# Gate convolution and output projection of a two-layer image block: which operand the matrix engine holds, and which it streams

## The chip, the cores and the metric

One Trainium2 chip, of which the kernel uses one core. The metric is the device time of one execution, in microseconds (us). Five timed runs of the kernel before are given, and one profiled execution of it. The engines are named as in the profile: PE is the matrix engine (PEld its loads of the stationary operand), DVE the vector engine, ACT the engine for activation functions, POOL a second vector engine, and SP issues nearly all DMAs.

## The reference

The input x has 16 images of 256 channels and 32 x 32 positions. Two layers act on each image, with residual connections and group norms around them. The first is attention (4 heads of 32) with a feed-forward part, the second is a selective scan over the 1024 positions, gated by a short convolution. Only the end of the second layer matters for this change:

```python
ctx = sigmoid(conv1d(xp, gate_w, padding=1) + gate_b)   # 3 taps, 256 -> 256 channels
...
y = scan(...) + u * D                                   # 512 channels, 1024 positions
y = y * silu(z)
x_mamba = y @ out_proj_w.T                              # 512 -> 256 channels
return (x_mamba * ctx).reshape(B, C, H, W)              # (positions, channels), read as (channels, H, W)
```

The last line is a bare reshape of an array of 1024 positions x 256 channels into 256 rows of 1024. Row r of the output therefore holds positions 4r to 4r + 3, each with its 256 channels. All matrix products here are in f32.

## The kernel before, in words

An SBUF or PSUM tile has 128 partitions. A matrix instruction holds a stationary tile (up to 128 x 128) in PE and streams a moving tile (up to 512 columns) through it; the columns of the stationary tile become the partitions of the result in PSUM. In the calls below the stationary operand is the second argument of `nc.tensor.matmul`, the moving one the third.

Activations lie with channels on partitions and positions along the tile. The gated result is wanted with position groups on partitions (row r has positions 4r to 4r + 3). So the kernel before makes every fourth position of the activations the stationary operand, 128 of them at a time (`ds(first, P, 4)`), and streams the weights, 256 output channels wide. The result comes out with positions on partitions. This is done in two places. `gate(o, hf, q, k)` (L707) convolves: three taps for each half of the input channels, then a one-row product that adds the bias (L713), then a tanh on ACT, and `g` is written to the DRAM tile `gs`. The sigmoid is taken as 0.5 (1 + tanh(x / 2)). `gate_and_store` (L887) does the output projection: four products, one for each 128 of the 512 channels, for each of eight groups of 128 positions, into the PSUM tile `m_ps`. `finish` then multiplies on DVE by (1 + g) (L874) and adds a quarter of the product to the residual `xs` (L876); the quarter holds both halves, of the sigmoid and of the silu. A finished row block goes to `out` by DMA.

The scan is the main loop. It has 4096 units, 256 for each image. Unit n runs one scan of 128 x 1024 on DVE (`scan`, L950), whose decay `a` was made two units ahead by two small products on PE (L942) and an exponential on ACT (L944), and whose input `dub` was multiplied on POOL (L933). There are two PSUM buffers for `a`, so the products for unit n + 2 wait until scan n has ended. `outputs` contracts each finished group of eight units on PE (`yb`, L975, and the turn at L987). Everything else is side work, written as generators that yield a share; between units the loop advances the side work by about one step of share 1 to 1.5. While image b is scanned, the side work is: the first norm of image b + 1 and the loads for the gate of image b - 1, then `gate_and_store(b - 1)`, then the attention and the scan inputs of image b + 1. `scan_inputs` holds the gate convolution: for each of four blocks d, two taps of the depthwise convolution on DVE (L693) with a projection `u_ps` on PE (L679), then four steps that each hold one call of `gate`. On each engine the instructions run in the order in which the program wrote them. SP's queue is separate and in order.

PSUM tiles come from few banks: `psum3` goes round three (two of pool `mm`, one of `accp`). `hwork` takes one of four SBUF tiles of 128 x 512, which the norms and the scan inputs use too.

Of the kernel before, what the change touches and what calls it, by code (L numbers as in the profile page):

```python
# [50 lines left out]
def attention_then_scan_kernel(  # L51
# [91 lines left out]
    gate_b = const.tile([1, C], F32, name="gate_b")  # L143
    nc.sync.dma_start(gate_b, gate_bias)
    one_row = const.tile([1, P], F32, name="one_row")
    nc.vector.memset(one_row, 1.0)
# [467 lines left out]
    def scan_inputs(b):  # L614
# [84 lines left out]
        def gate(o, hf, q, k):  # L699
            if (hf, q, k) == (0, 0, 0):  # L700
                gates["g"] = work("g")
            if (q, k) == (0, 0):
                gates["ps"] = psum("g_ps")
            g, ps = gates["g"], gates["ps"]
            first = o * HL + hf * 2 + q
            for t in range(3):
                nc.tensor.matmul(  # L707
                    ps[:, ts(q, C)], xp[k][:, ds(first + t, P, 4)], wg_s[:, k, t, :],
                    start=(k == 0 and t == 0), stop=False,
                )  # L710
            if k < KC - 1:
                return
            nc.tensor.matmul(ps[:, ts(q, C)], one_row, gate_b, start=False, stop=True)  # L713
            if q == 1:
                table("tanh")
                nc.scalar.activation(g[:, hs(hf)], ps, AF.Tanh, scale=0.5)
# [8 lines left out]
        for d in range(ND):  # L725
# [8 lines left out]
            gate(d // 2, d % 2, 0, 0)  # L734
            yield 1
            gate(d // 2, d % 2, 0, 1)
# [4 lines left out]
            gate(d // 2, d % 2, 1, 0)  # L741
            yield 1
            gate(d // 2, d % 2, 1, 1)
# [107 lines left out]
    def gate_and_store(b):  # L851
# [18 lines left out]
        ready = []  # L870

        def finish():
            for o, hf, ps in ready:
                nc.vector.scalar_tensor_tensor(ps, gs[o][:, hs(hf)], 1.0, ps, ALU.add, ALU.mult)  # L874
# [4 lines left out]
            ready.clear()  # L879

        for o in range(KC):
            for hf in range(2):
                ps = psum3("m_ps")
                for q in range(2):
                    first = o * HL + hf * 2 + q
                    for d in range(ND):
                        nc.tensor.matmul(  # L887
                            ps[:, ts(q, C)], us[d][:, ds(first, P, 4)], wo_s[:, d, :],
                            start=(d == 0), stop=(d == ND - 1),
                        )  # L890
                    if q == 1:
                        finish()
                    if come:
                        come.pop(0)()
# [252 lines left out]
```

## Time and profile before

| what | value |
|---|---|
| median of five runs | 12741.91 us |
| lowest and highest of the five | 12673.7 and 12773.79 us |
| the profiled execution | 12770.75 us, its span 12769.0 us |
| DVE busy | 11316.9 us, of which scans (L950) 9204.3 us |
| POOL busy | 10014.4 us |
| PE busy | 9939.5 us |
| gate products (L707), busy on PE | 461.1 us (tile `g_ps`), bias rows (L713) 87.3 us |
| output projection (L887), busy on PE | 320.6 us |
| mean granted clock of PE | 0.796 |

The profile is of one execution. Busy time is the union of an engine's instructions, so overlapped records count once. A granted clock of 1.00 is PE's full speed, and 0.50 half. Idle time of an engine says what it waited for, not that the wait costs run time: an engine that is not the bound may wait for nothing. Times in the timeline are microseconds from the start of the span.

### The profile page before, as it was taken

What the parts mean: (1) busy time and instruction counts of PE and PEld (TensorE: products, weight loads), DVE (VectorE), ACT (ScalarE), POOL (GpSimd) and SP (SyncE); (2) the same over time, 40 slices, a digit from 0 to 9 for tenths busy, and PEclk for the clock granted to TensorE, in tenths of its full rate; (3) what the DMA queues carried; (4) which work ended last, traced back from release to release, by engine and by line L of the source; (5) the groups of instructions that cost most, each with busy time, mean ns of one, the idle gap of its engine ahead of it and who ended that gap; (6) DMA issues with size and microseconds to landing.
All of it is one profiled execution on the core that took longest, in us unless ns stands there. A gap on an engine that the chain in (4) does not pass through costs nothing.

```text
span 12769.0 us, 424578 instructions
## 1 busy us (share of the span) xinstructions
PE 9939.5 (78%) x186800; PEld 5503.2 (43%) x186800; DVE 11316.9 (89%) x7480; ACT 7505.2 (59%) x10726; POOL 10014.4 (78%) x4201
## 2 busy tenths in 40 slices
PE   6676977868788787986878778697786878868777
PEld 2344444444444444444444444444444444444444
DVE  2789999989989899798998999999998998989998
ACT  3565665656556565465656656565565665656554
POOL 0587878878788787687878878787887878878798
PEclk8787988869788787687878878797787978878756
DMA  1567666676666766467666676666767667676676
GB/s 54 184 218 242 213 221 237 221 243 214 220 239 220 244 220 231 174 218 247 218 224 235 220 239 219 236 221 215 235 222 244 212 220 240 214 246 208 228 251 229
DMA packets 1038404, 2820.12 MB, mean 221 GB/s; under 512 B 290370, under 2 KB 368451, under 8 KB 1036548
## 3 DMA queue, kind: packets, MB, share of 16 engines
q1 hardware_dynamic: 1036548, 2792.97, 64.0%
q8 instruction: 1459, 23.90, 0.8%
q14 instruction: 397, 3.25, 0.1%
HBM read 2513.82 MB, written 261.62 MB: 217 GB/s over the span
## 4 chain that ended last, share of the span: by engine, by line
PE 40%; DVE 29%; issue 12%; ACT 8%; DMA 6%; POOL 3%; SPq 1%; DVEq 0%; POOLq 0%; ACTq 0%
DVE h L950 22%; PE yb L975 8%; PE s_ps L449 7%; PE a L942 6%; ACT a L944 4%; DMA dub<-dus 3%; PE av L508 3%; POOL dub L933 3%; PE st_ps L520 3%; PE yb L987 2%; PE z_ps L657 2%; PE g_ps L707 2%; PE m_ps L887 2%; DVE u L693 1%; DMA xs<-ud 1%
## 5 line engine op out<-in xcount | busy, mean ns | idle before, releaser
L933 POOL TENSOR_TENSOR dub<-dub,bt 128x1024 f32<-128x1024 f32 x4096 | 9789.1, 2420 | 2625.4 <-DMA dub<-dus 2457.4
L950 DVE TENSOR_TENSOR_SCAN h<-a,dub 128x1024 f32<-128x1024 f32 x4096 | 9204.3, 2276 | 721.9 <-ACT a L944 410.2
L944 ACT ACTIVATE a<-a,acol 128x1024 f32<-128x1024 f32 x4096 | 4464.1, 1090 | 3083.7 <-PE a L942 2957.7
L975 PEld LDWEIGHTS yb<-h,cd 128*32 128x32 f32 x131072 | 2509.7, 129 | 2688.3 <-issue 1304.2
L942 PE MATMUL a<-pieces,pick 48*128 48x512 bf16 x8192 | 1915.4, 459 | 2228.3 <-DVE h L950 2113.0
L975 PE MATMUL yb<-h,cd 128*32 128x64 f32 x131072 | 3282.5, 253 | 339.3 <-ACT y L981 231.8
L942 PEld LDWEIGHTS <-pick 48*128 48x128 bf16 x8192 | 570.9, 95 | 2636.4 <-issue 2226.2
L981 ACT COPY y<-yb 128x256 f32<-128x256 f32 x2048 | 763.9, 373 | 742.9 <-PE yb L975 734.5
L508 PE MATMUL av<-pt,vv 128*64 128x512 f32 x2048 | 606.4, 673 | 2.6 <-ACT sums L497 1.7
L528 ACT ACTIVATE pt<-st_ps 128x512 f32<-128x512 f32 x1024 | 553.8, 597 | 76.9 <-PE st_ps L520 75.8
L987 PE MATMUL yb<-turn,y 128*32 128x16 f32 x32768 | 590.9, 214 | 4.3 <-issue 3.3
L520 PE MATMUL st_ps<-sp 33*128 33x512 f32 x2048 | 586.1, 648 | 3.3 <-ACT pt L528 3.3
L449 PE MATMUL s_ps<-kd,q 32*64 32x512 f32 x2044 | 565.5, 641 | 17.1 <-DVE mx L428 9.0
L987 PEld LDWEIGHTS yb<-turn,y 128*32 128x32 f32 x32768 | 572.9, 159 | 5.3 <-issue 3.6
L449 PE MATMUL s_ps<-k,q 32*64 32x512 f32 x2048 | 540.5, 615 | 0.0
L991 ACT COPY yo<-yb 128x128 f32<-128x128 f32 x512 | 135.7, 265 | 594.5 <-PE yb L987 586.2
L428 DVE CUSTOM_DVE_ANT_0 over<-s_ps,over 128x512 f32<-128x512 f32 x512 | 343.3, 672 | 137.5 <-issue 60.4
L707 PE MATMUL g_ps<-w,xp 128*128 128x256 f32 x1464 | 461.1, 455 | 0.0
L707 PEld LDWEIGHTS g_ps<-w,xp 128*128 128x128 f32 x1464 | 370.2, 326 | 69.0 <-issue 58.6
L454 ACT ACTIVATE over<-s_ps 128x512 f32<-128x512 f32 x511 | 303.5, 594 | 60.5 <-PE s_ps L449 60.5
L693 DVE SCALAR_TENSOR_TENSOR u<-up,cwh,u 128x1024 f32<-128x1024 f32 x192 | 312.9, 1630 | 28.0 <-ACT u L685 27.7
L887 PE MATMUL m_ps<-w,xs 128*128 128x256 f32 x1024 | 320.6, 463 | 10.9 <-POOL xs L862 10.9
(178 smaller groups left out, 7110.0 us busy)
## 6 DMA issues: line engine op xcount, KB each, us to landing
dub<-dus SPq DMA_DIRECT2D x4096, 512.0 KB
dps<-pc SPq DMA_DIRECT2D x384, 128.0 KB
pieces<-dps SPq DMA_DIRECT2D x1024, 48.0 KB
xs<-in_x_dram SPq DMA_DIRECT2D x64, 512.0 KB
xs<-kept SPq DMA_DIRECT2D x64, 512.0 KB
zs<-z SPq DMA_DIRECT2D x64, 512.0 KB
ud<-u SPq DMA_DIRECT2D x64, 512.0 KB
dus<-du SPq DMA_DIRECT2D x64, 512.0 KB
```

The source lines that it names most:

```text
L449: nc.tensor.matmul(s[ts(e, 64)], q4[r, ts(c, 64)], keys[r], start=True, stop=True)
L508: nc.tensor.matmul(av[ts(e, 2 * DH)], vv[j // (NJ // 2)][:, j % (NJ // 2), 2 * pair + e, :], pts[e], start=(j == 0), stop=(j == NJ - 1),)
L520: nc.tensor.matmul(s, ka[r, ts(j, P)], qa[r, hs(hf)], start=True, stop=True)
L707: nc.tensor.matmul(ps[:, ts(q, C)], xp[k][:, ds(first + t, P, 4)], wg_s[:, k, t, :], start=(k == 0 and t == 0), stop=False,)
L887: nc.tensor.matmul(ps[:, ts(q, C)], us[d][:, ds(first, P, 4)], wo_s[:, d, :], start=(d == 0), stop=(d == ND - 1),)
L933: nc.gpsimd.tensor_tensor(v, v, blocks[units[n][0]]["bt"], ALU.mult)
L942: nc.tensor.matmul(a[:, hs(hf)], w, pieces[r], start=True, stop=True)
L944: nc.scalar.activation(a, a, AF.Exp, scale=acol[:, at : at + 1])
L950: nc.vector.tensor_tensor_scan(now["h", e][:, i, :], decays.pop(n), loaded.pop(n), 0.0, ALU.mult, ALU.add)
L975: nc.tensor.matmul(yb[ts(g, 32), ts(s, 64)], cd[:, at // 16, ts(c, 32)], hbuf[:, :, at : at + 8], start=(c == 0), stop=(c == 1),)
L981: nc.scalar.copy(y2[:, r], yb[:, :256])
L987: nc.tensor.matmul(some[ts(r, 32), x], y2[:, r, x:256:8], turn[:, x], start=True, stop=True)
```

## The change

In both places the operands are exchanged. The weights become the stationary operand and 512 neighbouring positions are streamed, so that results come out with channels on partitions. In the gate this halves the number of products, and the bias becomes a column that ACT adds within the tanh, halved beforehand because the activation's scale of 0.5 does not reach the bias. `gs` then holds channels on rows. In the output projection each step projects 512 positions to 128 channels; `join` multiplies by (1 + g) on DVE into an SBUF tile, still by channels; `turn_back` takes every fourth position of two joined tiles as the stationary operand and streams a 128 x 128 identity, which puts position groups on partitions; `finish` adds the quarter to the residual. The eight steps of the stage keep their yields; four are now projections and four are turns, in a written order.

```diff
@@ -140,10 +140,9 @@
         assert i + n <= w
         return vec[:, o + i : o + i + n]
 
-    gate_b = const.tile([1, C], F32, name="gate_b")
-    nc.sync.dma_start(gate_b, gate_bias)
-    one_row = const.tile([1, P], F32, name="one_row")
-    nc.vector.memset(one_row, 1.0)
+    gate_b = const.tile([P, KC], F32, name="gate_b")
+    nc.sync.dma_start(gate_b, gate_bias.rearrange("o (k p) -> p (o k)", p=P))
+    nc.vector.tensor_scalar(gate_b, gate_b, 0.5, None, ALU.mult)
     ident = const.tile([P, P], F32, name="ident")
     make_identity(nc, ident)
     avg = const.tile([P, P], F32, name="avg")
@@ -696,24 +695,22 @@
 
         gates = {}
 
-        def gate(o, hf, q, k):
-            if (hf, q, k) == (0, 0, 0):
+        def gate(o, hf, part):
+            if (hf, part) == (0, 0):
                 gates["g"] = work("g")
-            if (q, k) == (0, 0):
+            if part == 0:
                 gates["ps"] = psum("g_ps")
             g, ps = gates["g"], gates["ps"]
-            first = o * HL + hf * 2 + q
-            for t in range(3):
+            for at in ((0, 1), (2,), (3, 4), (5,))[part]:
+                k, t = divmod(at, 3)
                 nc.tensor.matmul(
-                    ps[:, ts(q, C)], xp[k][:, ds(first + t, P, 4)], wg_s[:, k, t, :],
-                    start=(k == 0 and t == 0), stop=False,
+                    ps, wg_s[:, k, t, ts(o, P)], xp[k][:, ds(hf * HL + t, HL)],
+                    start=(at == 0), stop=(at == 5),
                 )
-            if k < KC - 1:
-                return
-            nc.tensor.matmul(ps[:, ts(q, C)], one_row, gate_b, start=False, stop=True)
-            if q == 1:
-                table("tanh")
-                nc.scalar.activation(g[:, hs(hf)], ps, AF.Tanh, scale=0.5)
+            if part == 3:
+                nc.scalar.activation(
+                    g[:, hs(hf)], ps, AF.Tanh, scale=0.5, bias=gate_b[:, o : o + 1]
+                )
                 if hf == 1:
                     nc.sync.dma_start(gs[ts(o, P), :], g)
 
@@ -731,16 +728,16 @@
             tap(d, 2)
             table("tanh")
             nc.scalar.activation(ups[d][:, :L], us[d], AF.Tanh)
-            gate(d // 2, d % 2, 0, 0)
+            gate(d // 2, d % 2, 0)
             yield 1
-            gate(d // 2, d % 2, 0, 1)
+            gate(d // 2, d % 2, 1)
             yield 1.5
             nc.vector.scalar_tensor_tensor(us[d], ups[d][:, :L], 1.0, us[d], ALU.add, ALU.mult)
             ups[d] = None
             nc.sync.dma_start(ud[ts(d, P), :], us[d])
-            gate(d // 2, d % 2, 1, 0)
+            gate(d // 2, d % 2, 2)
             yield 1
-            gate(d // 2, d % 2, 1, 1)
+            gate(d // 2, d % 2, 3)
             yield 1.5
         gates.clear()
         del xp, body
@@ -867,35 +864,54 @@
                 yield 0.4
         if b + 2 < B:
             come += fetches(state[b + 2].setdefault("tok", []), state[b + 2]["kept"])
-        ready = []
+        turned, gated = [], {}
 
         def finish():
-            for o, hf, ps in ready:
-                nc.vector.scalar_tensor_tensor(ps, gs[o][:, hs(hf)], 1.0, ps, ALU.add, ALU.mult)
+            for o, hf, ps in turned:
                 t = xs[o][:, hs(hf)]
                 nc.vector.scalar_tensor_tensor(t, ps, 0.25, t, ALU.mult, ALU.add)
                 if hf == 1:
                     nc.sync.dma_start(out[b, ts(o, P), :], xs[o])
-            ready.clear()
-
-        for o in range(KC):
-            for hf in range(2):
-                ps = psum3("m_ps")
-                for q in range(2):
-                    first = o * HL + hf * 2 + q
-                    for d in range(ND):
-                        nc.tensor.matmul(
-                            ps[:, ts(q, C)], us[d][:, ds(first, P, 4)], wo_s[:, d, :],
-                            start=(d == 0), stop=(d == ND - 1),
-                        )
-                    if q == 1:
-                        finish()
-                    if come:
-                        come.pop(0)()
-                    yield 1.3
-                ready.append((o, hf, ps))
+            turned.clear()
+
+        def project(o, k):
+            ps = psum3("m_ps")
+            for d in range(ND):
+                nc.tensor.matmul(
+                    ps, wo_s[:, d, ts(k, P)], us[d][:, hs(o)],
+                    start=(d == 0), stop=(d == ND - 1),
+                )
+            return ps
+
+        def join(o, k, ps):
+            v = gated[o, k] = hwork("v")
+            nc.vector.scalar_tensor_tensor(v, gs[k][:, hs(o)], 1.0, ps, ALU.add, ALU.mult)
+
+        def turn_back(o, hf):
+            ps = psum3("o_t")
+            for q in range(2):
+                for k in range(KC):
+                    nc.tensor.matmul(
+                        ps[:, ds(q * C + k * P, P)], gated[o, k][:, ds(hf * 2 + q, P, 4)], ident,
+                        start=True, stop=True,
+                    )
+            turned.append((o, hf, ps))
+
+        work_on = [("p", 0, 0), ("p", 0, 1), ("p", 1, 0), ("t", 0, 0), ("p", 1, 1), ("t", 0, 1), ("t", 1, 0), ("t", 1, 1)]
+        joined = []
+        for what, o, i in work_on:
+            for j in joined:
+                join(*j)
+            joined.clear()
+            finish()
+            if what == "p":
+                joined.append((o, i, project(o, i)))
+            else:
+                turn_back(o, i)
+            if come:
+                come.pop(0)()
+            yield 1.3
         finish()
-        del ps
         yield 1
         state[b].clear()
```

## The prediction

> **What bounds the kernel now.** I read the page's busy shares first, then its chain of waits, then the table by stages for the two places that the change touches, then the timeline inside them, and at last single tiles for what one record costs. A matrix instruction in f32 shows as two weight-load records and two matmul records; I count records.
>
> ```profile
> PE 9939.5 (78%) x186800; PEld 5503.2 (43%) x186800; DVE 11316.9 (89%) x7480; ACT 7505.2 (59%) x10726; POOL 10014.4 (78%) x4201
> ...
> PE 40%; DVE 29%; issue 12%; ACT 8%; DMA 6%; POOL 3%; SPq 1%; DVEq 0%; POOLq 0%; ACTq 0%
> ```
>
> DVE is the busiest engine (4096 scans of 2.28 us), yet the chain lies more on PE. Each is the bound in some stages, so the stages decide. The table by stages, for one output projection (8305.22 on) and one stretch of gate and u (8009.25 on), with a third stretch for later use; the columns are length, then busy time of PE, PEld, DVE, ACT, POOL, the granted clock, and DMA:
>
> ```profile
> 5202.00:5365.00 163.00, 163.00 (x1558) 56.66 (x1548) 90.21 (x93) 58.90 (x81) 74.99 (x32) 0.50 0.31 111
> 8305.22:8332.73 27.51, 24.70 (x452) 18.01 (x451) 25.00 (x18) 12.18 (x16) 19.60 (x9) 1.00 0.67 208
> 8009.25:8087.00 77.75, 65.75 (x1099) 44.31 (x1098) 75.13 (x38) 40.93 (x55) 57.99 (x23) 0.93 0.61 201
> ```
>
> In the gate stretch DVE is idle for 77.75 - 75.13 = 2.6 us only: whatever PE saves there, no more than 2.6 us a batch can come of it. In the output projection the two are level in this view, so its timeline must tell (start, duration, instruction, PE alone):
>
> ```profile
> 8305.22 2.24 PE L887 MATMUL m_ps<-w,xs 128*128 128x256 f32 x8
> 8307.39 0.65 PE L975 MATMUL yb<-h,cd 128*32 128x64 f32 x32
> 8307.98 0.39 PE L942 MATMUL a<-pieces,pick 48*128 48x512 bf16 x2
> 8308.30 2.24 PE L887 MATMUL m_ps<-w,xs 128*128 128x256 f32 x8
> 8310.47 0.65 PE L975 MATMUL yb<-h,cd 128*32 128x64 f32 x32
> ```
>
> No row has an idle mark: PE runs back to back, 3.08 us from one projection step to the next (8305.22 to 8308.30), in order, and the `a` that the scan needs stands behind the projection step. DVE needs 2.28 + 0.69 = 2.97 us a step on average (two 0.7 us operations in every second step). This stage is PE's: there PE time is run time. One cycle is 2.17 us for the eight projection records (8305.22 to 8307.39) and 0.91 us for the rest.
>
> **What a record costs.** The gate and the u projection stand side by side; below them are the weight loads of m_ps, v_ps and u_ps (minimum/median/maximum ns):
>
> ```profile
> 8009.26 1.78 PE L707 MATMUL g_ps<-w,xp 128*128 128x256 f32 x6
> 8010.96 0.69 PE L713 MATMUL g_ps<-gate_b,one_row 1*128 1x256 f32 x2
> 8011.59 0.65 PE L975 MATMUL yb<-h,cd 128*32 128x64 f32 x32
> ...
> 8012.49 1.99 PE L679 MATMUL u_ps<-xp,w 128*128 128x512 f32 x4
> 8014.40 0.31 PE L975 MATMUL yb<-h,cd 128*32 128x64 f32 x7
> ...
> L887 PEld LDWEIGHTS m_ps<-w,xs x1024: 307/330/333, 1256.0 to 12762.8; 128*128 128x128 f32 x171
> ...
> L482 PEld LDWEIGHTS v_ps<-w,xn x512: 186/192/338, 119.1 to 11584.3; 128*128 128x128 f32 x171
> ...
> L679 PEld LDWEIGHTS u_ps<-xp,w x512: 186/189/337, 295.9 to 11928.4; 128*128 128x128 f32 x171
> ```
>
> A gate call of three instructions holds PE for 8010.96 - 8009.26 = 1.70 us, its bias row for 0.63. The u projection is the after form (weights held, 512 positions streamed): 1.91 us for two instructions (8012.49 to 8014.40); single records follow at 0.43 us, so four instructions take 1.91 + 4 x 0.43 = 3.63 us. Loads taken from every fourth element (m_ps, g_ps) last 330 ns, loads from neighbouring elements (v_ps, u_ps) 190; m_ps records follow at 0.233 us where half of a 0.427 us record of 512 would be 0.213. I read the difference as the strided load setting the pace.
>
> **Gate beside the scan, 15 stages.** Removed per block of 512: 4 calls x 1.70 + 2 bias rows x 0.63 = 8.1 us of PE. Added: 6 instructions of 512 in four parts, 2 x 1.91 + 2 x 1.05 = 5.9 us. Four blocks: PE saves 8.6 us a batch. DVE hides it: PE itself waits there for scans to free the `a` buffer (11.4 us of this stretch by the list of waits), so the gain lies between 0 and 2.6 us. I take 1.0, as the rest of the idle time also belongs to the u projections and to the waits after the yb rows: -15 (0 to -39). The tanh keeps its size; its bias comes from a column, at no cost. The step order, the yields and so the pacing of the side work stay as they are.
>
> **Gate of the first batch, alone.** No scan runs. PE goes back to back through bias and gate rows with one 1.4 us wait for ACT per block. A block takes two times 3.10 us for twelve gate records (306.38 to 309.48) and 0.63 for a bias row, 7.45 us; after it, 12 records at 0.43 with a lead of 0.1 are 5.3. Four blocks: -8.6.
>
> **Output projection beside the scan, 14 stages.** Eight steps stay eight steps. Four become projections of 512: 3.63 for 2.17, +1.46 each, +5.8 a batch. Four become turns: 4 instructions, 8 records, whose stationary tile is again every fourth element. Two rows bound a turn: v_ps (128 columns streamed, neighbouring stationary, 16 records in 1.99 us) gives 1.0 us for eight, m_ps (the same strided load) gives 2.17. I take the latter, as the load form is the same: no gain. Even at 1.0 little comes of it, as DVE's 2.97 us then sets the step (-0.1 each), though a lone projection behind a turn could hide up to 1.5 us in the two `a` buffers. So +4 to +5.8, and +6.9 if all records cost their means over both clock states (u_ps 266.5 us/512 = 0.52 a record); I take +5.0: +70 (+56 to +97). DVE's own work is unchanged: four joins of about 0.7 us replace four multiplications of 0.67, four finishes stay. The turn waits for its joins, but these stand a step earlier on DVE; the third join, issued in the step of the first turn, is needed three steps later. Behind a turn that waited would stand yb and `a`, and so the scan.
>
> The Trainium skill prices this differently. TensorE: Matmul & The Clock Gate, section LDWEIGHTS, gives a load by its column count alone (128/1.2 = 107 ns), which would make a turn about 1.0 us; SBUF — State Buffer, section Door 1, has 16-byte lines and a penalty where each access meets a new line, and every fourth f32 is just that, which agrees with 330 against 190 ns. By the first the sum below would be about 6 us lower, by the second it stands. Perfetto Trace Analysis, section Transposes, speaks against turning with a standard matmul, which this change does; no row here shows a transpose instruction.
>
> **The last batch.** Its eight projection steps lie far apart at half clock: one took 3.73 us (12228.61 to 12232.34) and DVE then idled 2.38 us. At half clock a projection of 512 takes 8 x 0.85 + 0.1 = 6.9 us, +3.2 for each of four, and a turn some 2.1, -1.6 for each: +7 (0 to +14). **The tail** after the last scan: 58 records took 15.7 us (12747.78 to 12763.5) behind the last product on POOL; now 26 records of 0.43 and 32 of 0.233 make 18.7, less one final DVE operation: +3 (0 to +6). **The start**: gate_b arrives as 256 single values, and one small DVE operation takes a memset's place: 0 to +2, taken as 0.
>
> **Sum.** -15 - 8.6 + 70 + 7 + 3 = +56 us. The profiled run took 12770.75 us (span 12769.0); it lies 0.2% above the median of the five, 12741.91, and I add the difference to the median: 12798. The bounds: -39 - 8.6 + 56 = +8, and -8.6 + 97 + 14 + 6 + 2 = +110.
>
> **Rivals.** (1) *The clock turns it round: not slower.* In 5202 to 5365 PE was busy all the time and the clock stayed at 0.50: 31 scans came 5.16 us apart, where other batches need about 3.05; that stretch cost some 65 us, in one batch of sixteen. If the denser 512 streams bring PE to the following stages at full clock and no such stretch remains, the time is 12798 - 65 = 12733, and with the low bounds of the rest 12685. It decides as soon as one such stretch is gone. Against it: the score stage comes long after, and half clock appears at many places. By the skill (TensorE: Matmul & The Clock Gate, HAM oscillation) idle gaps throttle the clock; this stretch has no idle time on PE. (2) *The clock goes the other way.* PE gets emptier in the gate stage, and one more such stretch appears: 12798 + 65 = 12863. (3) *A late gate tile.* The second half of gs was issued about 7 us ahead of the first projection and was needed seven steps later; now the second join, on DVE and in front of scans, needs it after two steps. Waits for DMAs were up to 3.9 us in the output projection's list: 3 us x 14 = +42, 12840. Against it: 7 us plus two steps of 4.5 us is ample. (4) *PE's saving in the gate counts in full*, as the chain's 2% for g_ps might suggest: 15 x 8.6 = 129 off instead of 15, 12684. DVE's 2.6 us speak against it; it goes with rival 1 as the other side.
>
> **How the numbers follow.** Forecast 0.47, the faster rivals (1 and 4) 0.30, rival 2 0.13, rival 3 0.10. About 0.5% (64 us: 12678 to 12806) can be told from no change. The forecast's own range, 12750 to 12852, straddles that bound: a bit over half of it counts as same, the rest as slower. Half of the faster rivals is beyond 0.5%. So slower 0.42, same 0.43, faster 0.15. The range 12700 to 12890 leaves out the ends of rivals 1, 2 and 4.
>
> **What would show it.** Right: the projection step's eight records take 3.6 us, turn loads 330 ns, PE idle in the output projection near nothing and DVE idle there up by 5 us a stage; the gate's stretch shorter by 1 us at most with PE idle up by 8. Wrong: turns near 1.0 us with the stage no longer than 28 us, joins that wait for gs, or a gate stretch shorter by over 3 us; and half-clock stretches of over 100 us more or fewer than one.

## The result, and the profile after

| kernel | timed executions | median us | lowest to highest us | profiled execution us |
|---|---|---|---|---|
| before | 94 | 12730.73 | 12617.02 to 12862.2 | 12770.75 (span 12769.0) |
| after | 54 | 12729.05 | 12630.94 to 12911.54 | 12678.48 (span 12676.7) |

The ratio of after to before is 0.9994, with a 95% interval from 0.998 to 1.0008: no difference that can be told, -8 us with an interval from -25 to +10. The forecast was +56. Two effects of some 50 to 80 us cancel, and one of them was forecast at 15. (Ratios, here and below, leave out executions that are over 1.5% slower than the fastest of their kernel; medians do not.)

The page of the kernel after, busy times and the chain of waits by engine:

```profile
PE 9812.0 (77%) x185776; PEld 5157.5 (41%) x185776; DVE 11234.7 (89%) x7480; ACT 7514.8 (59%) x10726; POOL 10069.7 (79%) x4201
...
PE 39%; DVE 31%; issue 12%; ACT 8%; DMA 7%; POOL 3%; SPq 1%; DVEq 0%; POOLq 0%; ACTq 0%
```

DVE has the same 7480 instructions as before and is busy for 82 us less (11316.9 to 11234.7). POOL has the same 4201 and is busy for 55 us more. The gate has no DVE operation that could have been taken out, so instructions became shorter. That is the first sign that something was misread.

The table by stages (length, then PE, PEld, DVE, ACT, POOL busy, granted clock, DMA share, GB/s): the part of the score stage (the attention's products of queries and keys) that lay at half clock before, one output projection, and one stretch of gate and u:

```profile
5193.26:5283.13 89.87, 89.81 (x1560) 36.91 (x1558) 87.16 (x97) 55.48 (x82) 73.46 (x33) 1.00 0.57 198
8203.38:8236.30 32.92, 31.09 (x462) 19.42 (x460) 28.59 (x19) 12.52 (x17) 19.71 (x9) 0.95 0.62 199
7919.81:7990.40 70.59, 59.12 (x1082) 29.66 (x1084) 68.11 (x39) 41.75 (x56) 64.95 (x24) 0.95 0.68 223
```

Against the three lines of before: the score part has the same 31 scans in 89.9 instead of 163.9 us (the 163.00 shown lie just inside them), at granted clock 1.00 instead of 0.50. The projection is 5.4 us longer and DVE is idle in it for 4.3 us instead of 2.5. The gate stretch is 7.2 us shorter, while DVE's idle time is 2.5 us against 2.6: what shrank is DVE's busy time, from 75.13 to 68.11. PE's idle time in it stayed as well, 11.5 us against 12.0.

Scans are numbered alike in both kernels, so the time from scan to scan can be set side by side. A batch is the 256 units of one image. "Units 16 to 40" of a batch hold the projection and what follows it, "units 168 to 216" the gate and u. Differences of the two profiled executions, after less before:

| where | us |
|---|---|
| up to the first scan | -3.5 |
| first batch (units 168 to 216 alone: -12.8) | -13.6 |
| 14 batches, units 16 to 40 | +49.0 |
| 14 batches, units 168 to 216 | -86.3 |
| 14 batches, units 40 to 74 (the half-clock part) | -52.7 |
| 14 batches, all other units | +4.0 |
| last batch | +2.6 |
| after the last scan | +8.1 |
| sum (span 12769.0 to 12676.7) | -92.4 |

The pair of profiles overstates. The half-clock stretch is in one execution and not in the other, and comes and goes whatever the kernel (below). The gate stage of before may also have been slow in this one execution: experiment 2 has the same gate and a shorter stage. The timed executions decide the size, the profiles the place.

The projection, from the timeline of after (start, duration, instruction):

```profile
8203.38 3.70 PE L880 MATMUL m_ps<-xs,w 128*128 128x512 f32 x8
8207.01 0.65 PE L991 MATMUL yb<-h,cd 128*32 128x64 f32 x32
8207.12 0.69 DVE L888 SCALAR_TENSOR_TENSOR v<-xs,m_ps 128x512 f32<-128x512 f32 x1 [1.65 <-PE m_ps L880]
8207.92 2.13 PE L894 MATMUL o_t<-ident,v 128*128 128x128 f32 x8
8209.98 0.65 PE L991 MATMUL yb<-h,cd 128*32 128x64 f32 x32
```

Eight projection records take 3.63 us (8203.38 to 8207.01) and a turn 2.06 (8207.92 to 8209.98): the terms of the forecast, and no idle mark on PE. The join (the first row of DVE) waits 1.65 us for its projection.

In the gate stretch the DVE groups carry the answer (busy us, mean ns of one, then idle time before them). Before:

```profile
L693 DVE SCALAR_TENSOR_TENSOR u<-up,cwh,u 128x1024 f32<-128x1024 f32 x192 | 312.9, 1630 | 28.0 <-ACT u L685 27.7
L738 DVE SCALAR_TENSOR_TENSOR u<-up,u 128x1024 f32<-128x1024 f32 x64 | 123.7, 1932 | 18.6 <-ACT up L733 18.6
```

After:

```profile
L692 DVE SCALAR_TENSOR_TENSOR u<-up,cwh,u 128x1024 f32<-128x1024 f32 x192 | 260.5, 1357 | 28.0 <-ACT u L684 27.7
L735 DVE SCALAR_TENSOR_TENSOR u<-up,u 128x1024 f32<-128x1024 f32 x64 | 105.6, 1649 | 11.9 <-ACT up L730 11.9
```

The same 192 taps and 64 products of u, in the same shape, take 52.4 + 18.1 = 70.5 us less. The change touches neither. The timelines show why they can differ. Before, DVE and then POOL:

```profile
8007.94 2.29 DVE L950 TENSOR_TENSOR_SCAN h<-a,dub 128x1024 f32<-128x1024 f32 x1 [0.24 <-ACT a L944]
8010.15 3.14 DVE L693 SCALAR_TENSOR_TENSOR u<-up,cwh,u 128x1024 f32<-128x1024 f32 x1
...
8009.85 2.36 POOL L933 TENSOR_TENSOR dub<-dub,bt 128x1024 f32<-128x1024 f32 x1 [1.32 <-DMA dub<-dus]
```

After, DVE and then POOL:

```profile
7919.36 1.30 DVE L692 SCALAR_TENSOR_TENSOR u<-up,cwh,u 128x1024 f32<-128x1024 f32 x1
...
7922.80 1.25 DVE L692 SCALAR_TENSOR_TENSOR u<-up,cwh,u 128x1024 f32<-128x1024 f32 x1
...
7926.18 1.25 DVE L692 SCALAR_TENSOR_TENSOR u<-up,cwh,u 128x1024 f32<-128x1024 f32 x1
...
7917.23 14.74 POOL L949 TENSOR_TENSOR dub<-dub,bt 128x1024 f32<-128x1024 f32 x5
```

Before, the tap came 0.30 us after POOL had begun. It ended at 8013.29, 1.08 us after POOL (8012.21), as if it had begun only then: 3.14 us where a free one takes 1.25. After, each tap begins as a product of POOL is ending (the first at 7919.36, 2.13 us into one that began at 7917.23) and takes 1.25 to 1.30, and POOL pays: five products back to back in 14.74 us, 2.95 each instead of 2.36. A tap reads two operands from SBUF, as POOL's product does; a scan reads `a` from PSUM and lasts 2.28 us in both kernels. So DVE's busy time holds waits for POOL, and who waits depends on who is early.

The two pairs stand for many. Beside the scan there are 240 taps and products of u. In the profile of before 62 of them last over 2 us, in that of after 25; of the 96 of before that last over 1.34 us, 93 end 1.0 to 1.15 us after the product of POOL in which they began. The granted clock of the stage is no rival: 0.900 and 0.906 on average over units 168 to 216.

In one point the first pair is not typical. The scan ahead of it waited 0.24 us for `a`, but only 14 of the 62 long ones follow a scan that waited for `a`, and 14 of the 25 as well. What came down is the others, from 48 to 11. In 52 of the 62 POOL had begun its product straight from a wait for its DMA, in 12 of the 25; over units 168 to 216 POOL is idle for 29.6 us a batch before and 20.0 after. So long taps go with a POOL that is ahead and waits for data, short ones with a POOL that is behind and works back to back.

### The profile page after: what moved, and what is told of

It reads as the page before. It is cut to its first block, busy times and chain, and to the rows that moved or that the text cites. A ratio compares the mean times of both kernels' runs of the same rounds, so it can differ in the third digit from the quotient of the medians.

```text
span 12676.7 us, 422543 instructions
## 1 busy us (share of the span) xinstructions
PE 9812.0 (77%) x185776; PEld 5157.5 (41%) x185776; DVE 11234.7 (89%) x7480; ACT 7514.8 (59%) x10726; POOL 10069.7 (79%) x4201
## 4 chain that ended last, share of the span: by engine, by line
PE 39%; DVE 31%; issue 12%; ACT 8%; DMA 7%; POOL 3%; SPq 1%; DVEq 0%; POOLq 0%; ACTq 0%
DVE h L966 23%; PE s_ps L448 7%; PE yb L991 7%; PE a L958 5%; ACT a L960 4%; DMA dub<-dus 3%; PE av L507 3%; POOL dub L949 3%; PE st_ps L519 3%; PE m_ps L880 2%; PE z_ps L656 2%; PE yb L1003 2%; DVE u L692 1%; PE qk_ps L412 1%; DMA xs<-ud 1%
## 5 line engine op out<-in xcount | busy, mean ns | idle before, releaser
L991 PEld LDWEIGHTS yb<-h,cd 128*32 128x32 f32 x131072 | 2481.5, 128 | 2793.9 <-issue 1373.9
L991 PE MATMUL yb<-h,cd 128*32 128x64 f32 x131072 | 3248.5, 251 | 337.0 <-ACT y L997 230.0
L706 PE MATMUL g_ps<-xp,w 128*128 128x512 f32 x732 | 410.2, 673 | 0.0
L692 DVE SCALAR_TENSOR_TENSOR u<-up,cwh,u 128x1024 f32<-128x1024 f32 x192 | 260.5, 1357 | 28.0 <-ACT u L684 27.7
L880 PE MATMUL m_ps<-xs,w 128*128 128x512 f32 x504 | 277.0, 699 | 9.4 <-POOL xs L859 8.6
L656 PE MATMUL z_ps<-xp,w 128*128 128x512 f32 x508 | 277.9, 674 | 1.4 <-ACT z_t L662 1.4
```

The source lines that it names most:

```text
L656: nc.tensor.matmul(ps, win_s[:, k, ds(DI + d * P, P)], body[k][:, hs(hf)], start=(k == 0), stop=(k == KC - 1),)
L991: nc.tensor.matmul(yb[ts(g, 32), ts(s, 64)], cd[:, at // 16, ts(c, 32)], hbuf[:, :, at : at + 8], start=(c == 0), stop=(c == 1),)
```

## The experiments

Four explanations are at stake. **The cap**, the forecast's: the gate gives at most 2.6 us a batch, and any more in the profiles is the clock's or chance. **The collision**: PE's work in the gate steps decides, perhaps by whether `a` comes in time, whether DVE's two-operand instructions begin behind POOL's products or clear of them, and the stage shrinks by more than DVE's idle time. For the projection, **the full stage**: PE, which is full there, is all of the cost. Its rival: the join's wait in front of the scans, or the strided loads of the turn.

The expectations, quoted as they were written, use letters that change from one to the next. "Theory A" is in 1 and 2 that the two halves are independent, in 4 to 7 the collision, in 9 that the gate's gain can be had without the loss; the cap stands in 1 as "my step". "Theory C" in 11 is that the bias rows alone made the gain. "Theory B" is the full stage throughout.

The results in one table. Ratios are to before, on the same chip; kernels without one had a single execution. The next two columns are means over the batches of the profiled execution (15 gate stages, 14 projections), in us, then the mean of the taps in ns, and the half-clock stretches of over 140 us in that execution.

| kernel | median us | ratio (95%) | units 168 to 216 | units 16 to 40 | tap ns | stretches |
|---|---|---|---|---|---|---|
| before | 12730.73 | | 155.3 | 76.8 | 1630 | 1 |
| after | 12729.05 | 0.9994 (0.998 to 1.0008) | 148.7 | 80.3 | 1357 | 0 |
| 1 gate only | 12610.46 | 0.9944 (0.9915 to 0.9973) | 147.1 | 77.3 | 1295 | 0 |
| 2 projection only | 12813.13 | 1.0072 (1.0033 to 1.0112) | 151.1 | 80.7 | 1450 | 2 |
| 3 turn from planes | 12811.65 | 1.007 (1.0029 to 1.0111) | 147.8 | 81.1 | 1302 | 1 |
| 4 gate refilled | 12790.84 | one, before 12778.41 | 152.4 | 80.3 | 1457 | 1 |
| 5 no bias rows | 12581.74 | one, before 12778.41 | 147.9 | 77.0 | 1339 | 0 |
| 6 before, no POOL product | 12332.38 | one | 143.4 | 76.5 | 1262 | 0 |
| 7 after, no POOL product | 12346.84 | one | 141.6 | 79.8 | 1261 | 0 |
| 8 projections spread | 12945.47 | 1.0195 (1.0152 to 1.0237) | 150.3 | 74.2 | 1472 | 0 |
| 9 gate turned | 12624.19 | 0.9963 (0.9928 to 0.9999) | 149.5 | 76.8 | 1346 | 2 |
| 10 gate turned, spread | 13179.25 | 1.035 (1.0288 to 1.0412) | 154.2 | 72.2 | 1573 | 5 |
| 11 bias rows in bf16 | 12669.32 | 0.9995 (0.9957 to 1.0033) | 149.1 | 77.0 | 1379 | 2 |
| 12 join a step later | 12754.98 | 1.0038 (1.0005 to 1.007) | 148.8 | 80.7 | 1346 | 2 |

**1 and 2: the two halves of the change.** Experiment 1 takes the new gate with the old `finish` and projection; experiment 2 the old `gate`, with bias rows, and the new projection:

```diff
 # 1, against before
-                    ps[:, ts(q, C)], xp[k][:, ds(first + t, P, 4)], wg_s[:, k, t, :],
...
+                    ps, wg_s[:, k, t, ts(o, P)], xp[k][:, ds(hf * HL + t, HL)],
...
-            nc.tensor.matmul(ps[:, ts(q, C)], one_row, gate_b, start=False, stop=True)
 # 2, against after
-                    ps, wg_s[:, k, t, ts(o, P)], xp[k][:, ds(hf * HL + t, HL)],
+                    ps[:, ts(q, C)], xp[k][:, ds(first + t, P, 4)], wg_s[:, k, t, :],
...
+            nc.tensor.matmul(ps[:, ts(q, C)], one_row, gate_b, start=False, stop=True)
```

> The gate of after (weights held, bias in the tanh) with the projection of before; the projection multiplies by g in a layout that does not belong to it, so the values mean nothing and only the time counts. Theory A, the two halves are independent and cancel: the gate stretch from the first to the last gate row stays at about 71 us (76.9 before), u taps at 1.36 us mean (1.63), the projection stretch at 27.6; the whole is faster by 15 x 5 + 3.5 = 75 to 90 us, ratio 0.993 to 0.994. Rival, my step that DVE's idle time caps the gate's gain: 0 to 39 us, ratio 0.997 to 1.000. Second rival, the u taps became shorter only because the projection shifted the phase of POOL and DVE: taps at 1.6 us here, ratio near 0.998.

> The projection of after (project, join, turn back) with the gate of before; g comes in the wrong layout, so only the time counts. Theory A: u taps back at 1.6 us, gate stretch about 77 us, projection stretch 33.4 us, the units after it 2 us shorter, the tail 8 us longer: slower by 14 x 3.7 + 8 + 3 = about 63 us, ratio 1.004 to 1.006. Rival, the parts are not independent and each alone is nothing: ratio 0.999 to 1.001.

The gate alone gives -0.56% (-71 us, -108 to -34), the projection alone costs +0.72% (+92 us, +42 to +143). Their sum of +21 has an interval of about 62 on either side (the two in quadrature), which holds the -8 of the whole change. The cap of 39 us, or 48 with the 8.6 forecast for the first batch, lies inside the interval of the gate's -71, so these times alone do not refute it; the stages and experiments 6 and 7 do. In experiment 2 the stage of the unchanged gate is 4.2 us shorter than before, with taps of 1450 ns where 1.6 us were expected: the entry into the stage also sets who is early. So of the 6.6 us between the two profiles the gate's own part is smaller. Kernels with the old gate have 155.3 and 151.1, those with the new one 148.7, 147.1, 147.8 and 148.8 (leaving out 4, 8, 9 and 10, in which the gate or the pace was changed further): 153.2 against 148.1, or 5.1 us x 15 = 77 us, near the 71 of the timed runs.

**3: the turn's loads.** The join writes four planes, each of neighbouring positions, and the turn loads a plane:

```diff
-            nc.vector.scalar_tensor_tensor(v, gs[k][:, hs(o)], 1.0, ps, ALU.add, ALU.mult)
+            by_four = lambda t: t.rearrange("p (x q) -> p q x", q=4)
+            nc.vector.scalar_tensor_tensor(
+                v.rearrange("p (q x) -> p q x", q=4), by_four(gs[k][:, hs(o)]), 1.0, by_four(ps),
+                ALU.add, ALU.mult,
+            )
...
-                        ps[:, ds(q * C + k * P, P)], gated[o, k][:, ds(hf * 2 + q, P, 4)], ident,
+                        ps[:, ds(q * C + k * P, P)], gated[o, k][:, ts(hf * 2 + q, P)], ident,
```

> After, with the joined tile written by planes (every fourth position together), so that the turn's stationary operand lies in neighbouring elements. If the strided load sets the turn's pace: loads 190 ns instead of 330, records 0.11 us apart instead of 0.233, a turn's eight records in about 1.1 us instead of 2.1. If PE's time is the run time of the projection stretch, the stretch falls by 4 x 1.0 = 4 us and the whole by 60 us (ratio 0.995); if DVE's 2.97 us per step take over in the turn steps, it falls by 0.5 us or less a stretch and the whole by under 10 us (ratio 0.999). Rival: the turn's pace is that of the matmul and the load is hidden; then nothing changes.

Weight loads of the turn (minimum/median/maximum ns), after and then experiment 3; below them experiment 3's join:

```profile
L894 PEld LDWEIGHTS o_t<-ident,v x512: 307/330/332, 1254.5 to 12671.2; 128*128 128x128 f32 x171
...
L898 PEld LDWEIGHTS o_t<-ident,v x512: 186/192/334, 1249.4 to 12800.6; 128*128 128x128 f32 x171
...
L889 DVE SCALAR_TENSOR_TENSOR v<-xs,m_ps x63: 1049/1098/1117, 1239.5 to 12791.4; 128x512 f32<-128x512 f32 x63
```

Only the stride was changed, and the load went from 330 to 192 ns; the records of a turn follow at 0.112 instead of 0.233 us, eight in 1.16 instead of 2.13. So the strided load set the pace of the turn, as the forecast read it. But the join, which now reads every fourth element, takes 1.10 instead of 0.69 us, and the stage is no shorter (81.1 against 80.3). PE work saved in the steps of the turns does not shorten the steps of the projections, which fill PE by themselves; but the four joins also cost DVE 1.6 us more a batch, and this run can't part the two. The whole is 0.7% slower than before, where 0.1 to 0.5% less was expected. Its stages account for about nothing of that (gate -77, units 16 to 40 +60, tail +5 us); its profile has one half-clock stretch of over 140 us and two shorter ones.

**4: PE work given back to the new gate.** Two of the six products of a block are done twice:

```diff
-            for at in ((0, 1), (2,), (3, 4), (5,))[part]:
+            for j, at in enumerate(((0, 1, 0), (2,), (3, 4, 3), (5,))[part]):
...
-                    start=(at == 0), stop=(at == 5),
+                    start=(part == 0 and j == 0), stop=(at == 5),
```

> After, with two of the six gate products of each block done twice (the sums are then wrong in these two terms), so that a block holds PE for 7.8 us, near the 8.1 of before, in the new form without strided loads or bias rows. Theory A, PE's time in the gate steps makes the scan late against POOL, and DVE's two-operand u operations then wait behind a POOL operation: u taps go back to 1.6 us mean (1.36 after, 1.63 before), the gate stretch to 75 us or more. Rival, the form of the operands (strided reads of the activations by PE) slowed DVE: taps stay at 1.36, the stretch at 71 to 73.

With some 2 us more a block on PE the stage goes from 148.7 to 152.4 and the taps from 1357 to 1457 ns, though DVE's instructions are those of after. The cap has no place for this; the collision has. The taps came back by a third of the way only (1.6 us were expected), so PE's time is not all that sets them.

**5: only the bias rows out.** The kernel before, whose gate leaves out the bias:

```diff
-                    start=(k == 0 and t == 0), stop=False,
+                    start=(k == 0 and t == 0), stop=(k == KC - 1 and t == 2),
...
-            nc.tensor.matmul(ps[:, ts(q, C)], one_row, gate_b, start=False, stop=True)
```

> Before, without the eight one-row bias products an image (the bias is left out): PE's time in a block falls from 8.1 to 6.8 us, the strided form stays. Theory A (PE time): taps between, 1.35 to 1.5 us, and half or more of the 5.5 us of the gate stretch comes off. Rival (form): taps at 1.6 us, stretch 76 us.

DVE's taps in experiment 5:

```profile
L693 DVE SCALAR_TENSOR_TENSOR u<-up,cwh,u 128x1024 f32<-128x1024 f32 x192 | 257.1, 1339 | 28.0 <-ACT u L685 27.7
```

Eight rows of 0.63 us, 5.0 us of PE a batch, are gone; the stage is 7.4 us shorter than that of before (155.3 to 147.9), or 5.3 shorter than the mean of the two kernels with the old gate: all that the new gate reaches. Holding the weights was not needed for it in this one execution.

**6 and 7: without the other party.** Both kernels without POOL's product (so `dub` lacks the factor `bt`):

```diff
-        nc.gpsimd.tensor_tensor(v, v, blocks[units[n][0]]["bt"], ALU.mult)
+        pass
```

> Before, with POOL's product of the scan input by B left out (the scan runs on what the DMA brought). Theory A: no POOL operation stands in DVE's way, all u taps take 1.25 to 1.3 us, the gate stretch falls from 76.9 to 72 us or less although PE does all its old work. Rival, POOL has no part in it: taps stay at 1.6 us mean, the stretch at 76 to 77.

> After, with the same product on POOL left out. Theory A: taps at 1.25 to 1.3 us here too; the gate stretch is shorter than in the kernel before without POOL's product by DVE's idle time alone, at most 2.6 us, not by the 5.5 us seen with POOL. Rival, PE bound the stretch of before: the difference stays at 5 us or more.

The taps of experiments 6 and 7, in this order:

```profile
L693 DVE SCALAR_TENSOR_TENSOR u<-up,cwh,u 128x1024 f32<-128x1024 f32 x192 | 242.2, 1262 | 28.0 <-ACT u L685 27.7
...
L692 DVE SCALAR_TENSOR_TENSOR u<-up,cwh,u 128x1024 f32<-128x1024 f32 x192 | 242.1, 1261 | 28.0 <-ACT u L684 27.7
```

With POOL idle the taps are equal, and the gate stage differs by 1.8 us instead of 6.6. That is within the forecast's cap of 2.6. The rest comes from POOL's product: these two runs show it, since they take POOL's part away and leave PE's saving in place. The projection's cost stays (76.5 to 79.8): it has nothing to do with POOL's product.

**8: more room for the projections.** In the kernel after the four projection steps count as 2.4 instead of 1.3:

```diff
-    GATE = ([0.6, 0.6, 0.4] * ND)[:-1] + [1.3] * 8 + [1]
+    GATE = ([0.6, 0.6, 0.4] * ND)[:-1] + [2.4, 2.4, 2.4, 1.3, 2.4, 1.3, 1.3, 1.3] + [1]
...
-            yield 1.3
+            yield 2.4 if what == "p" else 1.3
```

> After, with the four projection steps given a share of 2.4 instead of 1.3, so that each of them gets about two scan units; the other side work is packed a little closer. Theory B, the projection stretch loses time because PE is full there and the work is too dense: the loss of 3.7 us a batch around the stretch falls to 1 us or less, and without new losses elsewhere the whole gains about 40 us on after: ratio 0.995 to 0.998. Rival, the loss is the join that waits for its projection in front of a scan: spreading changes it little, ratio 0.999 to 1.001.

Units 16 to 40 get 6.1 us shorter, and the median batch goes from 772.9 to 780.8 us: units 74 to 168 of the 14 batches take 154 us more than before, as the side work that was pushed out makes them denser. The whole is 2% slower where a gain was expected. The projection's cost can't be paced away like this. With the gate of after unchanged, the taps rise from 1357 to 1472 ns (and from 1346 in experiment 9 to 1573 in 10): the pace of the side work changes the collision too.

**9 and 10: the gain without the loss.** The gate of experiment 9 holds the weights, ACT adds the bias and writes planes, an identity turns them, and the tanh follows; the projection is that of before, so `gs` has its old layout. Experiment 10 paces the old projection's steps at 2.0 in addition:

```diff
 # 9, against before
+                v = gates[o, k] = hwork("g_v")
+                nc.scalar.activation(
+                    v.rearrange("p (q x) -> p x q", q=4), ps.rearrange("p (x q) -> p x q", q=4),
+                    AF.Identity, bias=gate_b[:, k : k + 1],
                 )
...
+                        ps[:, ds(q * C + k * P, P)], gates[o, k][:, ts(hf * 2 + q, P)], ident,
 # 10, against 9
-                    yield 1.3
+                    yield 2.0
```

> Weights held in the gate, then the convolution's result copied by ACT with its bias into planes, turned by identity (16 products of 128 columns an image, neighbouring loads) and put through tanh into the layout of before; the projection as before. Theory A: the gate keeps most of its gain (PE 8.6 us less, about 4 us more for turns, ACT 4 x 0.6 us more), the projection loses nothing: ratio 0.993 to 0.996. Rival, the turns and the ACT copies delay the u taps or fill PE as before: ratio 0.998 to 1.001.

> The kernel with the turned gate (weights held in the gate, projection of before), with the eight projection steps given a share of 2.0 instead of 1.3. Theory B: DVE's 5 us of idle time around the projection stretch falls to 2 us, batches are 2 to 4 us shorter than with the turned gate alone; ratio 0.990 to 0.994. Rival, the closer packing of the rest costs as much: ratio 0.996 as without the spread.

Experiment 9 is 0.37% faster than before (0.9963, 0.9928 to 0.9999), the fastest of the kernels that leave nothing out, though its interval ends close to 1. Experiment 10 is 3.5% slower, against an expected 0.6 to 1% gain: its units 74 to 168 take 167 us more than before, its median batch is 784.5 us, and its profile has five half-clock stretches. The table by stages of 10, for one of them:

```profile
2867.00:3030.00 163.00, 163.00 (x1560) 56.83 (x1558) 90.76 (x94) 58.66 (x81) 74.85 (x33) 0.50 0.34 111
```

**11: smaller bias rows.** The kernel before with the bias as three bf16 rows that add up to it, in one product:

```diff
-            nc.tensor.matmul(ps[:, ts(q, C)], one_row, gate_b, start=False, stop=True)
+            nc.tensor.matmul(ps[:, ts(q, C)], one_rows, bias_rows, start=False, stop=True)
```

> Before, with the bias added by one bf16 product of three rows (the bias split into three bf16 parts) instead of an f32 product of one row; nothing else changed. Theory C, the bias rows alone were what the gate change gained by removing: the new product takes about 0.1 us more than its weight load instead of 0.63, the gate stretch falls to 70 or 71 us as without bias rows, taps at 1.35 us; ratio 0.991 to 0.995. Rival, any wait or row at this place costs the same: stretch 74 us or more, ratio 0.998 to 1.000.

The bias rows on PE, before and then experiment 11:

```profile
L713 PE MATMUL g_ps<-gate_b,one_row 1*128 1x256 f32 x244 | 87.3, 438 | 0.0
...
L720 PE MATMUL g_ps<-bias_rows,one_rows 3*128 3x256 bf16 x122 | 34.2, 280 | 0.0
```

PE is spared 53 us and the stage falls to 149.1, with taps of 1379 ns: the stage is as expected. The whole time is not: it can't be told from before's (0.9995, 0.9957 to 1.0033), where 0.991 to 0.995 was expected. The profile has two half-clock stretches, and the mean granted clock of its timed executions is lower (0.7967 against 0.7982); at one clock the gain shows (below).

**12: the join's wait.** In the kernel after all four projections come first and each join is written a step later:

```diff
-        work_on = [("p", 0, 0), ("p", 0, 1), ("p", 1, 0), ("t", 0, 0), ("p", 1, 1), ("t", 0, 1), ("t", 1, 0), ("t", 1, 1)]
+        work_on = [("p", 0, 0), ("p", 0, 1), ("p", 1, 0), ("p", 1, 1), ("t", 0, 0), ("t", 0, 1), ("t", 1, 0), ("t", 1, 1)]
...
+            if joined and joined[0][0] < n - 1:
+                join(*joined.pop(0)[1:])
```

> After, with the four projections first and each join one step later, so that no join stands on DVE in front of a scan while its projection is still running. PE's work is the same. Theory B, PE is full in the projection stretch: the wait of the joins (8.9 us an image) goes, but the scans then wait for their decay instead, and the 24 units around the stretch stay at 79 to 81 us (80.3 after, 76.9 before); ratio to before 0.998 to 1.001. Rival, the joins' wait is the loss: these units fall to 77 or 78 us, ratio 0.995 to 0.997.

The list of DVE's waits (total us, times, longest), after and then experiment 12:

```profile
DVE h L966 <- ACT a L960: 373.2, 415, 11.1
DVE v L888 <- PE m_ps L880: 137.5, 58, 5.4
...
DVE h L965 <- ACT a L959: 448.7, 461, 11.5
...
DVE v L888 <- PE m_ps L880: 41.1, 16, 9.8
```

The join's wait falls by 96 us and the scan's wait for `a` rises by 76 over the whole execution; in units 16 to 40 alone they go from 8.92 to 2.51 and from 3.18 to 7.87 us a batch, and the last operations come to wait 2.36 us for the turns. The stage stays (80.3 and 80.7). DVE waited for the same PE under another name: the full stage holds, and the join's wait is not the loss.

**All timed runs at one clock.** Each timed execution of the experiments, and of before beside them, has its mean granted clock on record. The 69 executions of before lie on a line: 132 us less for each 0.01 of clock, with a scatter of 15 us about it, and at clock 0.80 it passes through 12678 to 12680 us on each of three chips. The other kernels with twelve or more executions have slopes of 123 to 145 us. At 0.80 they lie off the line of before by -66 us (experiment 1), -54 (9), -43 (11), +16 (3), +37 (12), +112 (2) and +44 (after). So most of the spread between executions goes with the clock; what sets the clock of an execution is not known. The gate's gain is there in 11, and in 1 it is -66 with an interval of some 11 on either side, beyond the cap's 48. The two halves, -66 and +112, add up to the +44 of the whole.

These offsets are no prices where the projection is new. In units 16 to 40 the granted clock is 0.858 in the profile of after and 0.822 in that of before; over the span this is 0.003 of the mean, some 40 us on the line, so that after, 2 and 12 look about that much slower than they are.

## Why the prediction was right and wrong

**The failed step** is the gate beside the scan: "In the gate stretch DVE is idle for 77.75 - 75.13 = 2.6 us only: whatever PE saves there, no more than 2.6 us a batch can come of it." It gave -15 (0 to -39), or -24 with the first batch; experiment 1 measured -71 and the stages give 5.1 us a batch. The step took busy time for work. Some 0.37 us of each tap (1630 against 1262 ns) and 0.73 of each product of u (1932 against 1199) were waits for POOL, (192 x 0.37 + 64 x 0.73) = 118 us in all. The same page held the warning: a row with a mean of 1630 ns beside rows of the timeline at 1.25 and 3.14. Without POOL's product the gate saves 1.8 us a batch, within the step's 2.6 (experiments 6 and 7). That PE's work in the gate steps changes which of the two comes is shown by experiments 4, 5 and 11. By what path it does so stays open: most long taps follow a scan that had not waited for `a`. The last lines of the forecast named the sign of being wrong: a gate stretch shorter by over 3 us. They also had PE idle for 8 us more in it, where it stayed at 12.0 and 11.5.

**Rival 4**, PE's saving in full (-129, or -138 with the first batch), put the whole at 12684, which is nearer to 12729 than the forecast's 12798; but its gate lies 67 us from the measured -71, the forecast's -24 lies 47. It isn't a matter of PE's time alone: in experiments 6 and 7 the same saving brought 1.8 us a batch.

**The projection** was right in its mechanism: eight records in 3.63 us, strided loads of 330 ns, a turn near 2.1 us, the stretch from the first to the last of its records 27.7 to 33.4 us on average (+5.7; the raw sum had +5.8). It was mis-sized in the net: of 5.0 x 14 = 70 came 49.0 us (3.5 a batch; the other kernels with the new projection at its old pace have 79.8 to 81.1 in these units, those with the old one 76.5 to 77.3). Units 16 to 24 are 5.8 us longer, but in units 24 to 32 2.25 us come back: `finish` has one DVE operation left there instead of two (1.35 us), DVE idles 0.8 us less, and the joins ran earlier, in time in which DVE waited for PE anyway. This credit was missing from the sum. "DVE's own work is unchanged" was true of the amount and not of the place. The timed +92 of experiment 2 (42 to 143) holds both values.

**The joins.** "The turn waits for its joins" was considered, that the join waits for its own projection was not: 137.5 us in all. Experiment 12 shows that it costs nothing by itself. **Rival 3**, a late gate tile, did not come: the joins' waits end with their projections, and none is for `gs`.

**The small terms.** The last batch took +2.6 (forecast +7; its own terms, 4 x 3.2 - 4 x 1.6, make 6). The tail took +8.1 (forecast +3, up to +6). In it the joins stand one behind the other for their projections, which the sum of PE records left out:

```profile
12649.46 0.69 DVE L888 SCALAR_TENSOR_TENSOR v<-xs,m_ps 128x512 f32<-128x512 f32 x1 [4.59 <-PE m_ps L880]
12655.51 0.69 DVE L888 SCALAR_TENSOR_TENSOR v<-xs,m_ps 128x512 f32<-128x512 f32 x1 [5.36 <-PE m_ps L880]
12658.94 0.69 DVE L888 SCALAR_TENSOR_TENSOR v<-xs,m_ps 128x512 f32<-128x512 f32 x1 [2.75 <-PE m_ps L880]
```

The first scan came 3.5 us earlier (forecast -8.6). Over the kernels it came at 412 to 439 us where the gate's operands are the old ones and at 391 to 431 where they are the new. The means lie 14 us apart, on the forecast's side, but one execution each and this scatter do not test a term of 8.6.

**The clock** (rivals 1 and 2). The stretch of before was gone in the profile of after, which makes 74 us of the 92 between the spans (the forecast had 65 for it), and then other half clock in units 40 to 74 gave 21 back. Profiles of the twelve experiments have none to five such stretches. All 16 of over 140 us, in whatever kernel, begin at unit 43 or 47 of a batch, in the score stage. The timed runs of before alone lie up to 245 us apart. What sets a stretch off stays open; experiments 2, 3, 10 and 11 have a whole time that their stages don't account for, and the clock is the only visible candidate. That such a stretch came in any kernel because of its gate or projection is not shown.

**The sum, put right** with the measured terms: gate -71 (with the first batch), projection +49, last batch +3, tail +8: -11 us. The timed -8 lies 3 us from it, which is luck: the -71 alone is known to 37 us on either side. The measured 12729 is 69 us below the forecast of 12798: 11 of these lie in the base (12742 was the median of five executions, 12731 that of 94), the most in the gate (-24 forecast with the first batch, -71 measured) and the projection (+70, +49).

**The turn's loads and the collision.** The loads took 330 ns against 192 with nothing changed but the stride. This agrees with the Trainium skill's SBUF — State Buffer, section Door 1, which has a penalty where each access meets a new 16-byte line; that it is the line is not shown, as only a step of four elements was run. The 107 ns that the formula in TensorE: Matmul & The Clock Gate, section LDWEIGHTS, makes of 128 columns (an estimate) are reached by neither.

For the collision the row of the tap behind POOL (3.14 us, ending 1.08 after POOL) and, in the mean, those of POOL behind the taps (2.95 against 2.36 us) come first. The Trainium skill agrees with them: SBUF — State Buffer, section Who interferes with whom, states that a DVE instruction with two SBUF inputs contends with a GpSimd instruction that reads SBUF, and its section Summary: rules for kernel authors that the second one to issue blocks until the first finishes. The forecast did not look there, since no operation of the gate runs on DVE or POOL.

## What to carry to other kernels

Before an engine's idle time is taken as the cap on a gain, compare the mean of its instructions with the shortest of the same shape; if the mean is well above, the busy time holds waits, and work on a third engine can set who waits. A bias as a matrix product of one row cost as much here as a product over 128 rows of the same width, so in a stage where PE is late it is worth adding it elsewhere. In a stage that one engine filled, moving a wait gained nothing, and spreading the work out cost more in the next stage than it gained.

## What was not expected of the hardware

- A DVE instruction with two SBUF operands and POOL's product of two SBUF operands exclude each other for nearly the whole instruction: up to 3.14 us instead of 1.25 in the rows shown on DVE, or 2.95 instead of 2.36 on average on POOL; without POOL's products the taps fall to 1262 ns.
- A product over one row (1 x 256, f32) held PE as long as one over 128 rows would: 0.63 us for its two records, 438 ns each on average, against 455 ns for the gate's records over 128 rows. In bf16 it shows as one record of 280 ns.
- A DVE operation (the join of experiment 3) that reads every fourth element of both operands took 1.10 us instead of 0.69.
- PE can stay at granted clock 0.50 for over 160 us while it is busy all the time (163.00 of 163.00 us), and the same 31 scans pass in 89.9 us at 1.00.
